# LayerNorm outputs transposed once in float32, and split after the transpose, from the fourth unit on

## The chip, the cores and the metric

The kernel runs on one core of a Trainium2 chip. The metric is the device time of one execution in microseconds. The kernel before the change takes 1624.39 us, the median of three runs (1623.93 to 1625.12).

The engines are named as the profile names them: PE (TensorE, with PEld for its weight loads), DVE (VectorE), ACT (ScalarE), POOL (GpSimd), SP (SyncE, which issues the transfers).

## The reference

Input `x` is 8 batches of 1024 tokens with 256 features in float32. With `LN` a LayerNorm without scale or shift:

```
x = x + LN(attention(LN(x), Wq, Wk, Wv, Wo))
x = x + LN(ffn(LN(x), weight, alpha, bias))

attention: q = x @ Wq (16 heads of 16), k = x @ Wk and v = x @ Wv (4 heads of 16, each used by 4 heads of q),
           rotary embedding of q and k, softmax(q k^T / sqrt(256)) v, then @ Wo
ffn:       x @ (ternary(weight) * alpha)^T + bias, where ternary gives 1, 0 or -1
           by a threshold of 0.7 * mean(|weight|)
```

## The kernel before

**Units.** The 8192 tokens are 16 units of 512 tokens (`UT` = 4 tiles of 128), two to a batch. A unit has three kinds of work: a projection (`Project`: LayerNorm of `x`, transposes, products for q, k and v, rotary embedding), the scores (32 steps of 4 score tiles, `SPU` = 32), and a tail (`Tail`: normalizing, the product with `Wo`, two LayerNorms, the ffn, the output). While the scores of unit u run, the tail of unit u-1 and the projection of unit u+3 are put between them.

**Scores.** For each of 128 score tiles of a unit TensorE makes `se` (L673, keys by queries), from which ScalarE takes the exponential `e` (L694), and `sm` (L600, queries by keys), of which VectorE takes the maxima `mx` (L625) for a later part of the scores. The products `av` (L714) add up `e` times v. `se` has three PSUM banks (`ps_e`), `sm` two double banks (`ps_mx`), `av` one.

**Windows.** `window` (L1164) takes two or three score tiles, with as many `sm` matmuls between, then stage parts that are due, then the `av` matmuls of a window two back. A part that needs a bank (`banked`, L1093) takes it from the three of `se`. So the size is 2 when such a part is ready and 3 otherwise (`window_size`, L1105), and a window of two does one such part. The order on PE, DVE and ACT is the order in which the program writes it (`manual_schedule`, L1253); POOL's is chosen by the scheduler. Each engine takes its queue in order. The steps at which parts come due stand in the lists `P_PARTS` (projection) and `T_PARTS`, `W_PARTS` (tail) from L969 on; `W_PARTS` is used for the tails 12 to 14, which run beside the scores of units 13 to 15.

**Two parts of float32.** Products are made in float32r, with each operand given as a rounded high part and the rest as a low part; a product adds high times high, high times low and low times high (`product`, L297; the ffn's weights are exact and need two terms). `split_hi` (L155) rounds, `split_lo` (L161) subtracts.

**The LayerNorm outputs** have to be transposed for the products. There are two ways in the kernel before:

- `transposed` (L262): GpSimd makes high and low part (L157, L162) of the normalized tile `xn`; then each part is transposed by four float32r matmuls (L267) into a bank, and ScalarE copies the bank to `xt0`, `xt1` or `ot0`, `ot1` (L271). Part `x` of `Project` and of `Tail` does this; there are four such parts for a projection (two halves, two parts each) and four for a tail.
- `transposed_split` (L274): `xn` is transposed once in float32 by four matmuls (L279), ScalarE copies the bank whole (L284), and GpSimd makes high and low part of the copy. Part `xw` of `Tail`, in `W_PARTS` alone.

In a projection the parts come from `begin` (L359: statistics, `norm`, `hi`, `lo`), and the transposed tiles are read by the products `pkv` and `pq`. The buffer `hl` (tag in `qkp`, one buffer) holds first the two parts `xs` of the projection's LayerNorm, then `hlq`, the two parts of the rotated q, which are sent to DRAM as `dq`. In a tail `scale` (L787, L788) and `heads` prepare the product `pa` with `Wo`; `stats_x` (L833) normalizes and splits; the product of the ffn is `pf`.

Other helpers that the prediction names: `kt` rotates k on GpSimd once `k_rot` has come back from DRAM; `rotate` (L312 to L317) and the splits of q run there too; `pm` (L648) transposes the maxima, and `ml` (L657) takes their low part from that bank.

Of the kernel before, what the change touches and what calls it, by code (L numbers as in the profile page):

```python
# [8 lines left out]
F32 = mybir.dt.float32  # L9
F32R = mybir.dt.float32r  # L10
# [6 lines left out]
P = 128  # L17
# [11 lines left out]
def kernel(  # L29
# [29 lines left out]
    nc = tc.nc  # L59
# [4 lines left out]
    ND = D // P  # L64
    NK = S // P
    UPB = S // UQ
    NU = B * UPB
# [8 lines left out]
    work = ctx.enter_context(tc.tile_pool(name="work", bufs=2))  # L76
# [78 lines left out]
    def split_hi(eng, hi, src):  # L155
        if eng is nc.gpsimd:
            eng.tensor_scalar(hi, src, 1.0, 0.0, ALU.mult, ALU.add)  # L157
        else:
            nc.scalar.copy(hi, src)

    def split_lo(eng, lo, src, hi):  # L161
        eng.tensor_tensor(lo, src, hi.bitcast(F32), ALU.subtract)  # L162

    def split(eng, hi, lo, src, hi_eng=None):

        split_hi(hi_eng or eng, hi, src)
        split_lo(eng, lo, src, hi)
# [15 lines left out]
    def psum(shape, name, dtype=F32):  # L183
        if spare[0]:
            spare[0] += 1
            if spare[0] % 5 < 2:
                return ps_mx.tile(shape, dtype, tag="sm", name=name)
        return ps_e.tile(shape, dtype, tag="se", name=name)
# [4 lines left out]
    ffn = {}  # L193
# [37 lines left out]
    def ln_stats(src):  # L231

        n = src.shape[1]
        mv = small.tile([P, 2, 2], F32, tag="mv", name="mv")[:, :n]
        st = small.tile([P, 2, 6], F32, tag="bnst", name="bnst")
        for t in range(n):
            nc.vector.bn_stats(st[:, t, :], src[:, t, :])  # L237
        for t in range(n):
            nc.vector.bn_aggr(mv[:, t, :], st[:, t, :])  # L239
        sc = small.tile([P, 2, 2], F32, tag="lnsc", name="lnsc")[:, :, :n]  # L240
        nc.gpsimd.tensor_scalar(sc[:, 1, :], mv[:, :, 1], EPS, 1.0, ALU.add, ALU.mult)  # L241
        nc.gpsimd.tensor_tensor(sc[:, 1, :], sc[:, 1, :], mhalf[:, :n], ALU.pow)  # L242
        nc.gpsimd.tensor_scalar(sc[:, 0, :], mv[:, :, 0], -1.0, 0.0, ALU.mult, ALU.add)
        return mv, sc
# [17 lines left out]
    def transposed(src, tag, name, copy=nc.scalar.copy):  # L262

        pt = psum([P, ND, 2 * P], f"pt_{name}", F32R)
        for t in range(2):
            for c in range(ND):
                nc.tensor.transpose(  # L267
                    pt[:, c, t * P : (t + 1) * P], src[:, t, c * P : (c + 1) * P], ident_r
                )
        dst = work.tile([P, ND, 2 * P], F32R, tag=tag, name=name, bufs=2 if tag[0] == "x" else 1)  # L270
        copy(dst, pt.bitcast(F32))  # L271
        return dst

    def transposed_split(src, tag, name):  # L274

        pt = psum([P, ND, 2 * P], f"pt_{name}")
        for t in range(2):
            for c in range(ND):
                nc.tensor.transpose(  # L279
                    pt[:, c, t * P : (t + 1) * P], src[:, t, c * P : (c + 1) * P], ident  # L280
                )

        whole = work.tile([P, ND, 2 * P], F32R, tag="xt0", name=name).bitcast(F32)
        nc.scalar.copy(whole, pt)  # L284
        parts = [
            work.tile([P, ND, 2 * P], F32R, tag=f"{tag}{l}", name=f"{name}_{l}", bufs=1)
            for l in range(2)
        ]
        split(nc.gpsimd, *parts, whole)
        return parts  # L290

    TERMS = ((0, 0), (0, 1), (1, 0))
# [19 lines left out]
    def rotate(eng, x, cos, sin, t2):  # L312

        for dst, table in ((t2, sin), (x, cos)):
            eng.tensor_tensor(dst, x, table.unsqueeze(1).to_broadcast(list(x.shape)), ALU.mult)  # L315
        eng.tensor_tensor(x[:, 0], x[:, 0], t2[:, 1], ALU.subtract)
        eng.tensor_tensor(x[:, 1], x[:, 1], t2[:, 0], ALU.add)  # L317
# [5 lines left out]
    class Project:  # L323
# [3 lines left out]
        def __init__(self, u, eng):  # L327
            self.u, self.eng = u, eng
            self.b, self.half = divmod(u, UPB)
            self.xt, self.sc, self.hl = {}, {}, {}  # L330
            self.q_rot = None
            if u not in (1, 2):
                xn = qkp.tile([P, UT, D], F32, tag="xn", name=f"xn_{u}", bufs=2)
                xs = qkp.tile([P, 2, UT, D], F32R, tag="hl", name=f"xs_{u}")
                self.xn = [xn[:, 2 * p : 2 * p + 2, :] for p in range(2)]
                self.xs = [[xs[:, l, 2 * p : 2 * p + 2, :] for l in range(2)] for p in range(2)]
            else:
                self.xn = [
                    tailp.tile([P, 2, D], F32, tag=f"xn{p}", name=f"xn_{u}_{p}") for p in range(2)
                ]  # L340
                self.xs = [
                    [ep.tile([P, 2, D], F32R, tag="e", name=f"xs_{u}_{p}_{l}") for l in range(2)]
                    for p in range(2)
                ]
# [14 lines left out]
        def begin(self, p):  # L359
            self.stats(p)  # L360
            self.norm(p)
            self.hi(p)
            self.lo(p)

        def x(self, p, l):
            self.xt[p, l] = transposed(self.xs[p][l], f"xt{l}", f"xt{l}_{self.u}_{p}")

        def kv(self, p):

            if p == 0:  # L370
                self.pkv = psum([P, UQ], f"pkv_{self.u}")
            xt = [self.xt[p, l] for l in range(2)]
            product(self.pkv[:, self.tokens(p)], columns(wqkv_s, D, 2 * DK), xt)
            if p == 1:
                self.kv_t = qkp.tile([P, UQ], F32, tag="kv_t", name=f"kv_t_{self.u}")
                nc.scalar.copy(self.kv_t, self.pkv)
# [361 lines left out]
    class Tail:  # L738
# [16 lines left out]
        def copy(self, p):  # L755
            return nc.scalar.copy
# [47 lines left out]
                self.copy(p)(hl[:, 0], self.on[p])  # L804
            split_lo(self.eng(p), hl[:, 1], self.on[p], hl[:, 0])

        def x(self, p, l):
            self.xt[p, l] = transposed(self.hl[p][:, l], f"ot{l}", f"ot{l}_{self.u}_{p}")

        def xw(self, p):  # L810
            self.xt[p, 0], self.xt[p, 1] = transposed_split(self.on[p], "ot", f"ot_{self.u}_{p}")

# [20 lines left out]
        def stats_x(self, p):  # L833
            self.sc[p] = ln_stats(self.x1[p])
            self.norm(p)
            if not NU - 4 <= self.u < NU - 1:
                self.split(p)

        def stats_f(self, p):
# [25 lines left out]
    class LastTail(Tail):  # L865
# [55 lines left out]
        x = o  # L921
# [17 lines left out]
    def at(step, f, *args):  # L939
        assert step >= -START  # L940
        todo.setdefault(step, []).append((f, args))
# [22 lines left out]
    def load(u):  # L964
# [2 lines left out]


    P_PARTS = (  # L969
        (26, "begin", 0), (33, "x", 0, 0), (34, "x", 0, 1), (37, "begin", 1), (43, "x", 1, 0),  # L970
        (45, "x", 1, 1), (49, "kv_and_dram"), (51, "q", 0), (54, "kt"), (53, "v"), (55, "q", 1),
        (62, "q_to_dram"),
    )
    L_PARTS = (
# [5 lines left out]
    T_PARTS = (  # L980
        (1, "fetch"), (7, "invert"), (8, "scale", 0), (9, "scale", 1), (12, "attn", 0),
        (15, "attn", 1), (15, "stats_a", 0), (17, "stats_a", 1), (19, "stats_x", 0),
        (23, "stats_x", 1), (24, "x", 0, 0), (25, "x", 0, 1), (26, "ffn", 0), (27, "x", 1, 0),
        (29, "x", 1, 1), (31, "ffn", 1), (31, "stats_f", 0), (33, "stats_f", 1),
    )


    P_SECOND = (26, 33, 34, 37, 43, 45, 49, 51, 52, 53, 55, 57)
    T_FIRST = (6, 8, 11, 12, 14, 16, 16, 17, 20, 23, 24, 25, 26, 27, 29, 31, 31, 33)
    P_FIRST = (47, 51, 52, 54, 57, 58, 59, 60, 62, 61, 63, 64)  # L990

    W_PARTS = (
        (1, "fetch"), (7, "invert"), (8, "scale", 0), (9, "scale", 1), (12, "attn", 0),
        (15, "attn", 1), (15, "stats_a", 0), (17, "stats_a", 1), (19, "stats_x", 0),
        (22, "xw", 0), (23, "stats_x", 1), (26, "ffn", 0), (27, "xw", 1), (31, "ffn", 1),
        (31, "stats_f", 0), (33, "stats_f", 1),
    )
    T_LAST = (1, 3, 4, 5, 9, 10, 11, 14, 17, 19, 20, 22, 25, 27, 24, 28)

    warm = []  # L1000
# [60 lines left out]
    for u in range(3, NU):  # L1061
        start = SPU * (u - 4)
        steps = P_FIRST if u == 3 else P_SECOND if u == 4 else [k for k, *_ in P_PARTS]
        at(start + steps[0] - 6, load, u)
# [12 lines left out]
    for u in range(NU - 1):  # L1077
        start = SPU * (u + 1)
        at(start + 1, begin_tail, u)
        parts = T_PARTS if u < NU - 4 else W_PARTS  # L1080
        steps = {0: T_FIRST, NU - 2: T_LAST}.get(u, [k for k, *_ in parts])
        for k, (_, *p) in zip(steps, parts):
            behind = [behind_latest] if u == 0 and p[0] == "fetch" else []
            at(start + k, *behind, part, tails, u, *p)
# [244 lines left out]
```

## Time and profile before

| what | value |
| --- | --- |
| median of three runs | 1624.39 us |
| the profiled execution: its time and its span | 1625.2 us |
| mean granted TensorE clock | 0.997 |
| steady unit (scores of unit 10, from 1039.19) | 96.30 us |
| unit 13 (no projection beside it, float32 transposes in its tail) | 90.57 us |
| `mx<-sm` reductions: 128x1024 | 715 of 1217 ns |
| `mx<-sm` reductions: 128x512 | 586 of 680 ns |
| `e<-se` exponentials | 1996 of 603 ns |
| ACT copies of a transposed bank: L271 to `xt`, to `ot`; L284 | 592, 599, 600 ns |
| POOL high part (L157) and low part (L162) of 128x512 | 621 and 1285 ns |

The profile is one execution, taken instruction by instruction. Busy time counts instructions in flight, waits between them not. Matmuls overlap: those of `se` and `sm` use different halves of the array's rows and run side by side, so TensorE's busy share says little about how close it is to its limit. A timeline row gives the start in us from the start of the span, the duration, the engine, the line, the operation, output<-inputs, the shape and the number of instructions merged into it; a bracket gives the idle time before it and what ended that.

### The profile page before, as it was taken

How to read it: one execution, taken by the hardware profiler on the slowest of the kernel's cores; microseconds unless marked ns; L12 is line 12 of the kernel's file. 1: busy time of each engine (PE TensorE's matmuls, PEld its weight loads, DVE VectorE, ACT ScalarE, POOL GpSimd, SP SyncE). 2: the span in 40 equal slices, each digit the busy share in tenths (PEclk: the TensorE clock that was granted, in tenths of full speed). 3: DMA queues.
4: the chain of work that ended last, by engine and by line, in shares of the span. 5: the costliest groups of instructions: out<-in, count | busy, mean ns of one | idle time of the engine just before them, and what ended most of it. 6: DMA issues, size and time to landing. Idle time of an engine off the chain costs nothing.

```text
span 1625.2 us, 37184 instructions
## 1 busy us (share of the span) xinstructions
PE 1576.5 (97%) x14702; PEld 813.9 (50%) x14702; DVE 1397.1 (86%) x2046; ACT 1270.1 (78%) x2473; POOL 833.8 (51%) x1239
## 2 busy tenths in 40 slices
PE   8999999999999999999999999999999999999997
PEld 6544454454545545454554545455454554444444
DVE  7878888889898888989889898988989888999964
ACT  4667878778787887878788787887878787787774
POOL 5542365364744637455364845546474552333354
PEclk9999999999999999999999999999999999999999
DMA  4151525124151422514133151513314141131100
GB/s 140 53 88 46 113 70 96 57 77 99 57 109 47 102 63 59 120 57 97 59 83 77 57 128 39 105 54 83 79 57 97 46 107 45 42 75 34 43 15 27
DMA packets 86078, 117.98 MB, mean 73 GB/s; under 512 B 12088, under 2 KB 50808, under 8 KB 85752
## 3 DMA queue, kind: packets, MB, share of 16 engines
q1 hardware_dynamic: 85904, 115.60, 29.7%
q8 instruction: 116, 1.90, 0.5%
q14 instruction: 58, 0.48, 0.1%
HBM read 68.65 MB, written 45.88 MB: 70 GB/s over the span
## 4 chain that ended last, share of the span: by engine, by line
PE 81%; DVE 10%; POOL 3%; ACT 2%; issue 2%; DMA 1%; SPq 0%; POOLq 0%; ACTq 0%; DVEq 0%
PE av L714 29%; PE se L673 28%; PE sm L600 9%; DVE mx L625 8%; PE pa L301 3%; PE pq L301 3%; PE pf L301 2%; ACT e L694 2%; PE pt_xt L267 2%; PE pt_ot L267 1%; PE pkv L301 1%; PE pm L648 1%; DVE bnst L237 1%; POOL lnsc L242 0%; DMA x<-in_L_attn_x 0%
## 5 line engine op out<-in xcount | busy, mean ns | idle before, releaser
L625 DVE TENSOR_REDUCE mx<-sm 128x2 f32<-128x1024 f32 (+1 forms) x1301 | 1204.8, 975 | 183.6 <-PE sm L600 164.0
L694 ACT ACTIVATE e<-se 128x512 f32<-128x512 f32 x1996 | 1057.0, 603 | 220.9 <-PE sm L600 163.7
L600 PE MATMUL sm<-k_st,q_st 64*128 64x512 f32 x2048 | 746.5, 448 | 7.2 <-DVE mx L625 4.1
L673 PE MATMUL se<-q_st,k_st 64*128 64x512 f32 x2048 | 705.6, 441 | 18.4 <-ACT e L694 14.6
L714 PE MATMUL av<-e,v_aug 128*32 128x256 f32 (+3 forms) x8584 | 606.0, 378 | 0.0
L673 PEld LDWEIGHTS se<-q_st,k_st 64*128 64x128 f32 x2048 | 324.5, 184 | 396.6 <-ACT e L694 305.4
L600 PEld LDWEIGHTS sm<-k_st,q_st 64*128 64x128 f32 x2048 | 325.2, 184 | 66.4 <-DVE mx L625 44.9
L714 PEld LDWEIGHTS av<-e,v_aug 128*32 128x32 f32 x8584 | 193.5, 108 | 212.5 <-issue 148.9
L241 POOL TENSOR_SCALAR lnsc<-mv 128x2 f32<-128x2 f32 (+1 forms) x134 | 26.1, 195 | 333.1 <-DVE mv L239 326.6
L788 POOL TENSOR_TENSOR xn<-xn,a 128x512 f32<-128x512 f32 x30 | 38.4, 1282 | 135.3 <-DMA a<-d_rec 130.0
L242 POOL TENSOR_TENSOR lnsc<-lnsc,mhalf 128x2 f32<-128x2 f32 (+1 forms) x134 | 92.5, 690 | 0.9
L157 POOL TENSOR_SCALAR xs<-xn 128x512 fp32r<-128x512 f32 x27 | 16.8, 621 | 130.8 <-DMA dq<-hlq 129.5
L162 POOL TENSOR_TENSOR hl<-xn,hl 128x512 fp32r<-128x512 f32 x54 | 68.7, 1285 | 0.1
L253 POOL TENSOR_SCALAR xn<-x,lnsc 128x256 f32<-128x256 f32 x116 | 64.3, 562 | 2.3
L853 POOL TENSOR_TENSOR a<-a,bias_bc 128x512 f32<-128x512 f32 x30 | 38.4, 1279 | 51.9 <-ACT a L852 51.9
L301 PE MATMUL pa<-woh,hl 128*128 128x256 f32 x240 | 46.2, 294 | 1.1 <-ACT e L694 1.1
L237 DVE BATCH_NORM_STATS2 bnst<-x 128x6 f32<-128x256 f32 x124 | 46.0, 413 | 1.3 <-DMA x<-in_L_attn_x 1.3
L315 POOL TENSOR_TENSOR t<-q_rot,sin_q_sb 128x512 f32<-128x512 f32 x31 | 39.7, 1282 | 12.2 <-ACT q_rot L457 12.1
L237 DVE BATCH_NORM_STATS2 bnst<-a 128x6 f32<-128x256 f32 x120 | 44.5, 413 | 0.0
L301 PE MATMUL pq<-xt,wqkvh 128*128 128x256 f32 x256 | 44.1, 294 | 0.5 <-ACT e L694 0.5
L457 ACT COPY q_rot<-pq 128x512 f32<-128x512 f32 x32 | 18.7, 586 | 28.3 <-PE pq L301 28.3
L301 PEld LDWEIGHTS pa<-woh,hl 128*128 128x128 f32 x240 | 34.6, 189 | 12.1 <-issue 6.3
(164 smaller groups left out, 1333.0 us busy)
## 6 DMA issues: line engine op xcount, KB each, us to landing
q_st<-dq SPq DMA_DIRECT2D x90, 256.0 KB
dq<-hlq SPq DMA_DIRECT2D x60, 256.0 KB
d_av<-avsb SPq DMA_DIRECT2D x60, 256.0 KB
x<-in_L_attn_x SPq DMA_DIRECT2D x15, 512.0 KB
xn<-d_av SPq DMA_DIRECT2D x30, 256.0 KB
a<-d_rec SPq DMA_DIRECT2D x30, 256.0 KB
xr<-in_L_attn_x SPq DMA_DIRECT2D x15, 512.0 KB
out_x<-a SPq DMA_DIRECT2D x30, 256.0 KB
```

Of the source, the lines that this page charges most:

```text
L162: eng.tensor_tensor(lo, src, hi.bitcast(F32), ALU.subtract)
L237: nc.vector.bn_stats(st[:, t, :], src[:, t, :])
L242: nc.gpsimd.tensor_tensor(sc[:, 1, :], sc[:, 1, :], mhalf[:, :n], ALU.pow)
L253: eng.tensor_scalar(dst[:, t, :], src[:, t, :], sc[:, 0, t : t + 1] if eng is nc.gpsimd else mv[:, t, 0:1], sc[:, 1, t : t + 1], ALU.add i ...
L267: nc.tensor.transpose(pt[:, c, t * P : (t + 1) * P], src[:, t, c * P : (c + 1) * P], ident_r)
L301: nc.tensor.matmul(out, chunk(left[i], c), chunk(right[j], c), start=(k == 0), stop=(k == len(steps) - 1),)
L315: eng.tensor_tensor(dst, x, table.unsqueeze(1).to_broadcast(list(x.shape)), ALU.mult)
L600: scores = nc.tensor.matmul(sm[0][:, part, :], queries[rows], k_st[(u // UPB) % 3][rows, r2, ch * 512 : (ch + 1) * 512], start=True, stop= ...
L625: early[0] = nc.vector.tensor_reduce(mx[i][:, a, head_and_tile(i, r2, t), lo:n], sm[0][:, lo:n, :], AX.X, ALU.max).ins
L673: nc.tensor.matmul(sc if len(queries.shape) == 2 else sc.rearrange("p (j t) -> p j t", j=G), k_st[(i // G // UPB) % 3][rows, r2, kt * P : ...
L694: nc.scalar.activation(e, sc, AF.Exp, scale=1.0 / D**0.5)
L714: nc.tensor.matmul(av_ps[0][32 * r : 32 * r + 32, lo:hi], va[:, kt, r, :], es[i * NK + kt, r // 2, r % 2][:, lo:hi], start=(kt == 0 and lo ...
```

## The change

From projection 3 on, and in all tails but the last, the normalized tile is transposed once in float32 (`transposed_split`, part `xw`). ScalarE now copies the bank twice: rounded into the high part, and whole. The whole copy goes back into the memory of the tile that was transposed, viewed by its new axes, and not into a buffer of tag `xt0`. GpSimd then only subtracts. `begin` no longer splits; projections from the fourth on have no `xs`, so `hl` holds `hlq` alone there. `W_PARTS` becomes the list of all tails, and the projection's list has two `xw` parts in place of four `x` parts. In a tail the first transposes come due at step 22, where `x` had steps 24 and 25; the second at 27, where `x` had 27 and 29.

```diff
@@ transposed_split
-        whole = work.tile([P, ND, 2 * P], F32R, tag="xt0", name=name).bitcast(F32)
-        nc.scalar.copy(whole, pt)
         parts = [
-            work.tile([P, ND, 2 * P], F32R, tag=f"{tag}{l}", name=f"{name}_{l}", bufs=1)
+            work.tile(
+                [P, ND, 2 * P], F32R, tag=f"{tag}{l}", name=f"{name}_{l}",
+                bufs=2 if tag[0] == "x" else 1,
+            )
             for l in range(2)
         ]
-        split(nc.gpsimd, *parts, whole)
+        whole = src.rearrange("p (c t) d -> p c (t d)", c=ND)
+        nc.scalar.copy(parts[0], pt)
+        nc.scalar.copy(whole, pt)
+        split_lo(nc.gpsimd, parts[1], whole, parts[0])
         return parts
@@ Project.begin
             self.stats(p)
             self.norm(p)
-            self.hi(p)
-            self.lo(p)
...
+        def xw(self, p):
+            self.xt[p, 0], self.xt[p, 1] = transposed_split(self.xn[p], "xt", f"xt_{self.u}_{p}")
@@ Tail.stats_x
-            if not NU - 4 <= self.u < NU - 1:
+            if self.u == NU - 1:
                 self.split(p)
@@ P_PARTS
-        (26, "begin", 0), (33, "x", 0, 0), (34, "x", 0, 1), (37, "begin", 1), (43, "x", 1, 0),
-        (45, "x", 1, 1), (49, "kv_and_dram"), (51, "q", 0), (54, "kt"), (53, "v"), (55, "q", 1),
+        (26, "begin", 0), (33, "xw", 0), (37, "begin", 1), (43, "xw", 1),
+        (49, "kv_and_dram"), (51, "q", 0), (54, "kt"), (53, "v"), (55, "q", 1),
         (62, "q_to_dram"),
@@ T_PARTS
-        (23, "stats_x", 1), (24, "x", 0, 0), (25, "x", 0, 1), (26, "ffn", 0), (27, "x", 1, 0),
-        (29, "x", 1, 1), (31, "ffn", 1), (31, "stats_f", 0), (33, "stats_f", 1),
+        (22, "xw", 0), (23, "stats_x", 1), (26, "ffn", 0), (27, "xw", 1), (31, "ffn", 1),
+        (31, "stats_f", 0), (33, "stats_f", 1),
@@ first units
-    P_SECOND = (26, 33, 34, 37, 43, 45, 49, 51, 52, 53, 55, 57)
-    T_FIRST = (6, 8, 11, 12, 14, 16, 16, 17, 20, 23, 24, 25, 26, 27, 29, 31, 31, 33)
-    P_FIRST = (47, 51, 52, 54, 57, 58, 59, 60, 62, 61, 63, 64)
+    P_SECOND = (26, 33, 37, 43, 49, 51, 52, 53, 55, 57)
+    T_FIRST = (6, 8, 11, 12, 14, 16, 16, 17, 20, 22, 23, 26, 27, 31, 31, 33)
+    P_FIRST = (47, 51, 54, 57, 59, 60, 62, 61, 63, 64)
@@ main loop
-        parts = T_PARTS if u < NU - 4 else W_PARTS
+        parts = T_PARTS
```

More of the change, by code (lines that the diff above doesn't have):

```diff
@@ L333, in __init__ @@
                 xn = qkp.tile([P, UT, D], F32, tag="xn", name=f"xn_{u}", bufs=2)
+                self.xn = [xn[:, 2 * p : 2 * p + 2, :] for p in range(2)]
+            if u == 0:
                 xs = qkp.tile([P, 2, UT, D], F32R, tag="hl", name=f"xs_{u}")
-                self.xn = [xn[:, 2 * p : 2 * p + 2, :] for p in range(2)]
                 self.xs = [[xs[:, l, 2 * p : 2 * p + 2, :] for l in range(2)] for p in range(2)]
-            else:
+            elif u < 3:
                 self.xn = [
@@ L805, in split @@
             split_lo(self.eng(p), hl[:, 1], self.on[p], hl[:, 0])
-        def x(self, p, l):
-            self.xt[p, l] = transposed(self.hl[p][:, l], f"ot{l}", f"ot{l}_{self.u}_{p}")
         def xw(self, p):
@@ L982 @@
         (15, "attn", 1), (15, "stats_a", 0), (17, "stats_a", 1), (19, "stats_x", 0),
-        (23, "stats_x", 1), (24, "x", 0, 0), (25, "x", 0, 1), (26, "ffn", 0), (27, "x", 1, 0),
-        (29, "x", 1, 1), (31, "ffn", 1), (31, "stats_f", 0), (33, "stats_f", 1),
-    )
-    P_SECOND = (26, 33, 34, 37, 43, 45, 49, 51, 52, 53, 55, 57)
-    T_FIRST = (6, 8, 11, 12, 14, 16, 16, 17, 20, 23, 24, 25, 26, 27, 29, 31, 31, 33)
-    P_FIRST = (47, 51, 52, 54, 57, 58, 59, 60, 62, 61, 63, 64)
-    W_PARTS = (
-        (1, "fetch"), (7, "invert"), (8, "scale", 0), (9, "scale", 1), (12, "attn", 0),
-        (15, "attn", 1), (15, "stats_a", 0), (17, "stats_a", 1), (19, "stats_x", 0),
         (22, "xw", 0), (23, "stats_x", 1), (26, "ffn", 0), (27, "xw", 1), (31, "ffn", 1),
```

## The prediction

> **What bounds the kernel now.** First the page's shares, to see which engines are near full.
>
> ```profile
> span 1625.2 us, 37184 instructions
> PE 1576.5 (97%) x14702; PEld 813.9 (50%) x14702; DVE 1397.1 (86%) x2046; ACT 1270.1 (78%) x2473; POOL 833.8 (51%) x1239
> PE 81%; DVE 10%; POOL 3%; ACT 2%; issue 2%; DMA 1%; SPq 0%; POOLq 0%; ACTq 0%; DVEq 0%
> ```
>
> The third line is the chain of waits: TensorE carries 81% of it and VectorE 10%. But matmuls overlap, so 97% busy does not say that TensorE never waits. The stretches show what is behind it. The first two below are whole units of 32 steps in the steady part (the score units 10 and 13; unit 13 has no projection left to do).
>
> ```profile
> 1039.19:1135.49 96.30, 94.83 (x920) 48.73 (x916) 85.13 (x124) 78.21 (x153) 53.25 (x78) 1.00 0.32 78
> 1328.09:1418.66 90.57, 88.10 (x849) 42.50 (x846) 82.30 (x119) 72.44 (x142) 30.56 (x46) 1.00 0.25 56
> ```
>
> The columns are span, then busy time of PE, PEld, DVE, ACT, POOL. Unit 13 has far less matmul work, and still takes 90.57 us with VectorE busy for 82.30. So TensorE and VectorE bound the kernel by turns: VectorE while nothing but scores runs, TensorE where a stage's matmuls come between. Units 2 to 12 take 96.30 to 96.45 us each.
>
> By turns, because the work goes in windows: two or three `se` matmuls paired with as many `sm` matmuls, at most one stage part (if two), then the `av` group. I read a window in TensorE's timeline from its first `se` row to the next window's. Windows of three without a wait last 1.46 us (`av` of one 256-wide piece) or 1.68 (one of 384, or two pieces); over units 3 to 14 their mean is 0.20 longer, up to 2.40. There VectorE reduces without a break and TensorE waits for a bank. Where small windows with parts follow one another, VectorE starves:
>
> ```profile
> 1074.23 1.22 DVE L625 TENSOR_REDUCE mx<-sm 128x2 f32<-128x1024 f32 x1 [0.20 <-PE sm L600]
> 1076.22 1.23 DVE L625 TENSOR_REDUCE mx<-sm 128x2 f32<-128x1024 f32 x1 [0.76 <-PE sm L600]
> 1079.07 1.23 DVE L625 TENSOR_REDUCE mx<-sm 128x2 f32<-128x1024 f32 x1 [1.62 <-PE sm L600]
> 1080.77 4.68 DVE L625 TENSOR_REDUCE mx<-sm 128x2 f32<-128x1024 f32 x5 [0.47 <-PE sm L600]
> ```
>
> The windows of 1073.43 to 1079.96 hold a transpose, a product `pa` and another transpose; the brackets add up to 3.05 us of idle VectorE. The change takes out windows like these.
>
> **The change part by part, for a unit like 10** (tail 9 and projection 13 run in it).
>
> *Transposes.* Eight groups of four in float32r become four groups in float32. Groups of both kinds stand in TensorE's timeline, each followed by its `av` row:
>
> ```profile
> 1114.92 0.54 PE L267 MATMUL pt_ot<-ident_r,hl 128*128 128x128 f32 x4
> 1115.39 0.85 PE L714 MATMUL av<-e,v_aug 128*32 128x384 f32 x8
> ...
> 1396.16 0.66 PE L279 MATMUL pt_ot<-ident,xn 128*128 128x128 f32 x4
> 1396.75 0.86 PE L714 MATMUL av<-e,v_aug 128*32 128x256 f32 x16
> ```
>
> Start to start, 0.47 us (0.45 to 0.47 in others; I take 0.46) against 0.59. So 8 x 0.46 - 4 x 0.59 = **-1.32 us**. The weight loads of the two kinds take the same, 140 ns each by their groups (L267 and L279 for `pt_ot`).
>
> The Trainium skill (TensorE: Matmul & The Clock Gate, Weight-path perf modes) speaks against the float32 form: the fast weight load, about 2x as measured there, is used only for 128 weights of a type that is not FP32. If float32r counted as such a type, a load of float32 would take twice 140 ns; 16 loads would add 16 x 0.14 = 2.2 us to a unit, an estimate by that page, and the change would lose. The two equal rows decide against it here.
>
> *Windows.* In the instruction order of the changed kernel units 1 to 12 have 49 windows (30 of three, 19 of two) where the trace has 50 (28 and 22). A group of `av` takes 0.57 us with one 256-wide piece and 0.78 otherwise: 22 x 0.57 + 28 x 0.78 = 34.4 before, 19 x 0.57 + 30 x 0.78 = 34.2 after. Each window also pays at its start and its end about 0.1 us more between score pairs than inside (0.34 and 0.33 against 0.23). Together **-0.35 us**, -0.15 to -0.5.
>
> *What VectorE takes back.* Two windows more are of three, and those run at VectorE's pace: 2 x 0.20 = **+0.4 us**, from 0 (if each lands where VectorE is starved) to +1.0. Over the whole kernel the order has 7 more reductions, each a split of one into two: 7 x (2 x 0.680 - 1.217) = 1.0 us, inside these bounds.
>
> *The bank.* The transposes' bank, one of three for `se`, is now held for two ScalarE copies (0.59 and 0.60 us) instead of one, before the third `se` of the next window can have it. ScalarE's copies number the same: 8 per unit. In the two `pt_xt` windows at 1044.80 and 1048.40 the copy ends at 1046.89 and 1050.55; one copy more makes 1047.48 and 1051.14, against a third `se` at 1047.30 and 1050.67, which the longer transposes push 0.13 later: 0.05 and 0.34 us late. Queued behind these copies are the window's next exponentials. Four times 0.1 gives **+0.4**, 0 to 4 x 0.34 = +1.4.
>
> *GpSimd.* Four high-part copies (0.62) go per unit: 2.5 us. Subtractions (1.28) stay four, now behind the transposes. The wait `xs` <- DMA of `hlq` (12.3 us in this unit) goes with the shared buffer; GpSimd sits off TensorE's path there, so I count it at nothing, and next in line after it is `a` L853, ready early. But in the second half of the unit GpSimd is packed, and the tail's first transposes come earlier on TensorE (step 22 instead of 24, ahead of the second `pq`):
>
> ```profile
> 1099.14 0.73 POOL L315 TENSOR_TENSOR t2k<-k_rot,sin_kt_sb 128x256 f32<-128x256 f32 x1 [2.65 <-DMA k_rot<-d_k]
> ...
> 1108.01 1.11 POOL L253 TENSOR_SCALAR xn<-x,lnsc 128x256 f32<-128x256 f32 x2
> ```
>
> From the DMA's landing GpSimd works in one run until `xn` is there, at 1109.12, 19.5 us after the window with `pkv` began (1089.65). Summing the windows of the new order up to the transposes by the rows of before (3.23, 1.68, 1.63, 3.29, 1.68, 1.61, 2.0, 1.5, 1.75, and 0.67 inside the last) TensorE is there after 19.0. It would wait 0.5 us, and all behind it on its queue too, the second `pq` first. Part of that falls where VectorE sets the pace: **+0.2**, 0 to +0.8. The subtraction behind it is due for `pf`, nine to ten us later, and is hidden: the copies and the subtraction take 0.6 + 0.6 + 1.3. The projection's subtractions have three or more windows before `pkv` needs them. If that cover went, `pf` or `pkv` would wait on GpSimd.
>
> *SyncE* issues the same 737 transfers; only `hlq` of unit 3 goes out earlier. Nothing is late by it.
>
> Sum per unit: -1.32 - 0.35 + 0.4 + 0.4 + 0.2 = -0.67. The other ledger is VectorE's idle time, 11.2 us in the unit. Without the second transposes the cluster quoted above should keep 0.20 + 0.76 + 0.8 = 1.8 of 3.05; the pair of `pt_ot` windows (0.54 + 0.68 idle) becomes one beside `pq`: together with `ptv` and that `pq` 2.9 becomes 1.9; the first `pt_xt` pair gives 0.3. That is -2.5, and the same givebacks plus 4 x 0.13 for longer transposes make +1.1: -1.4. The ledgers bracket it; I take **-1.0 us per unit**. Units 1 to 12 have it: -12. Unit 0 has the projection of unit 3 alone: 4 x 0.46 - 2 x 0.59 = -0.7. Units 13 to 15 already transpose in float32, keep their 46, 47 and 42 windows, and trade a GpSimd copy for one on ScalarE: 0. Span 1625.2 - 12.7 = 1612.5. The span is 0.8 us above the median of 1624.39, so I forecast **1612 us**.
>
> **The rivals.**
> *A, the whole of it.* VectorE refills fully and no giveback comes: 2.2 us per unit, 26.4 + 0.7: 1597. For it: the idle ledger. Against it: the bank and `xn`.
> *B, swallowed.* Windows of three are already paced by VectorE, so TensorE's saving becomes waiting: for it unit 13: by the windows' shortest forms it has 78.6 us of TensorE against 89.5 in unit 10, and these 10.9 us less gave 5.7 us of time, in part because VectorE's busy time fell by 2.8. Against it: 11.2 us of idle VectorE, at windows that go. Then 1623.
> *C, slower.* GpSimd's run gets `xn` to the tail's first transposes late, and TensorE, in order, waits in each of 12 units. At the 0.2 us I take nothing turns; it decides from 1.2 us per unit on. At 2.2 us (the `k_rot` wait was up to 3.6 long against 2.65 here, one us more; one more if `pkv` is reached later by the chain than I sum) the unit grows by 1.0: 1624.4 + 12 - 0.7 = 1636. For it: the packed rows from 1099.14 on. Against it: the hand sum gives only 0.5.
> That the change does not do what it says is excluded by the instruction order: 16 float32 transposes stand per unit where 32 float32r stood.
>
> **How the numbers follow.** Forecast (1604 to 1619) 0.45, A 0.27, B 0.13, C 0.15. About 0.2%, 3.2 us, is what a measurement of this kernel can tell from no change: faster is 0.45 + 0.27 = 0.72, same 0.13, slower 0.15. The range goes from A to just beyond B, 1597 to 1625.
>
> **What would show it.** Per steady unit: span about 95.3; VectorE busy near 85 still, its idle near 10; four groups of L279-like transposes 0.59 from start to `av`; no wait of `xs` for `hlq`. Wrong, if `pt_ot` or `pf` waits for GpSimd by more than 1 us per unit (C), if the third `se` after transposes waits near 0.6 us for the second copy, or if the unit falls below 94.5 (A).

## The result and the profile after

The changed kernel takes **1633.3 us** (median of four, 1630.5 to 1634.1) against 1624.6 for the kernel before in the same session: ratio 1.0049, 95% interval 1.0035 to 1.0063. It is slower by 0.5%, more than the measurement's own uncertainty. The forecast was 1612.

First the same three lines of the page, after (its execution took 1630.5 us):

```profile
span 1628.6 us, 36757 instructions
PE 1573.8 (97%) x14470; PEld 797.0 (49%) x14470; DVE 1396.1 (86%) x2053; ACT 1272.5 (78%) x2479; POOL 805.0 (49%) x1183
PE 71%; DVE 20%; POOL 3%; issue 2%; DMA 2%; ACT 2%; SPq 0%; POOLq 0%; DVEq 0%; ACTq 0%
```

TensorE has 232 matmul records fewer and GpSimd 56 instructions fewer, as meant. But in the chain of waits VectorE's share went from 10% to 20%, and TensorE's from 81% to 71%: the chain now passes through VectorE more often. What that is worth in time the chain does not say; the units do. The two stretches of one unit each, after (score units 10 and 13):

```profile
1042.34:1138.76 96.42, 94.70 (x904) 47.48 (x901) 85.14 (x125) 78.17 (x153) 51.20 (x74) 1.00 0.32 78
1331.72:1422.29 90.57, 88.02 (x840) 42.24 (x836) 82.08 (x119) 73.10 (x144) 29.39 (x44) 1.00 0.26 57
```

Unit 10 was 96.30 and is 96.42. VectorE's idle time there was 96.30 - 85.13 = 11.17 and is 96.42 - 85.14 = 11.28: the forecast wanted 1.4 less. Unit 13 stayed, as forecast. The cluster that the prediction quoted, in VectorE's timeline after:

```profile
1077.57 1.23 DVE L631 TENSOR_REDUCE mx<-sm 128x2 f32<-128x1024 f32 x1 [0.20 <-PE sm L606]
1079.67 1.22 DVE L631 TENSOR_REDUCE mx<-sm 128x2 f32<-128x1024 f32 x1 [0.87 <-PE sm L606]
1082.53 4.68 DVE L631 TENSOR_REDUCE mx<-sm 128x2 f32<-128x1024 f32 x5 [1.64 <-PE se L679]
```

The brackets add up to 2.71 us (3.05 before; 1.8 forecast). The window with the second transposes is gone, but the 1.6 us of idle time after the product `pa` was never that window's: it stays and stands before the next window of three.

**By units.** I read each unit's length as the time from its first `se` to the next unit's (unit 0 from TensorE's first matmul, at 3.92 us in both):

| score unit | before | after | difference |
|---|---|---|---|
| 0 | 166.51 | 163.28 | -3.23 |
| 1 | 98.16 | 103.23 | +5.07 |
| 2 | 96.32 | 96.40 | +0.08 |
| 3 to 12 together | 963.18 | 964.88 | +1.70 |
| 13 and later | 297.1 | 296.9 | -0.2 |

So there are two questions: what costs 5 us in unit 1, and why the other eleven of the twelve units that should have gained 1 us each gained nothing. (Unit 0 turns out to be the clock's, see below; without its 3.2 us the spans would differ by 6.6 us, and the medians differ by 8.7; the two us between are within what executions of either kernel differ by.)

**Unit 1.** TensorE's timeline after has two long waits there, which the kernel before doesn't have:

```profile
192.68 0.47 PE L679 MATMUL se<-q_st,k_st 64*128 64x512 f32 x1 [3.67 <-DMA q_st<-ml]
...
242.50 0.98 PE L279 MATMUL pt_ot<-ident,xn 128*128 128x128 f32 x4 [2.56 <-POOL xn L253]
```

The first waits for the shift rows of job 5 (the maxima for one part of the scores, put beside the queries), which a DMA brings from `ml` into `q_st`. The timeline of SyncE's queue, after and then before, says what went out ahead of them:

```profile
177.23 6.62 SPq L496 DMA_DIRECT2D dq<-hlq  x4
185.12 1.48 SPq L670 DMA_DIRECT2D q_st<-ml  x2
```

```profile
188.05 1.39 SPq L664 DMA_DIRECT2D q_st<-ml  x2
...
211.45 4.55 SPq L490 DMA_DIRECT2D dq<-hlq  x4
```

The queries of unit 3 (four transfers of 256 KB) moved from behind the shift rows to just ahead of them. In the stretches 170 to 180 and 180 to 190 us the DMA engines are busy to 0.98 and 0.77 (before: 0.75 and 0.93). Why they moved stands in GpSimd's timeline of the kernel before:

```profile
210.22 1.20 POOL L157 TENSOR_SCALAR hlq<-q_rot 128x512 fp32r<-128x512 f32 x2 [1.33 <-PE pt_xt L267]
```

`hlq` of unit 3 could not be written before the transposes had read `xs` of projection 4, for both live in the one buffer `hl`. The change frees that buffer, GpSimd writes `hlq` at 169.2 to 177.4, and its transfers go out into engines that are full.

### The profile page after: what moved, and what is told of

Same layout as the page of the kernel before. It is cut to its first block, busy times and chain, and to the rows that moved or that the text cites. A ratio compares the mean times of both kernels' runs of the same rounds, so it can differ in the third digit from the quotient of the medians.

```text
span 1628.6 us, 36757 instructions
## 1 busy us (share of the span) xinstructions
PE 1573.8 (97%) x14470; PEld 797.0 (49%) x14470; DVE 1396.1 (86%) x2053; ACT 1272.5 (78%) x2479; POOL 805.0 (49%) x1183
## 4 chain that ended last, share of the span: by engine, by line
PE 71%; DVE 20%; POOL 3%; issue 2%; DMA 2%; ACT 2%; SPq 0%; POOLq 0%; DVEq 0%; ACTq 0%
PE av L720 25%; PE se L679 23%; DVE mx L631 17%; PE sm L606 9%; PE pa L305 3%; PE pq L305 3%; PE pf L305 2%; PE pkv L305 1%; ACT e L700 1%; DVE bnst L237 1%; PE pt_ot L279 1%; PE pt_xt L279 1%; PE pm L654 1%; DMA q_st<-ml 0%; DMA k_rot<-d_k 0%
## 5 line engine op out<-in xcount | busy, mean ns | idle before, releaser
L679 PE MATMUL se<-q_st,k_st 64*128 64x512 f32 x2048 | 712.9, 443 | 10.2 <-ACT e L700 4.2
L720 PE MATMUL av<-e,v_aug 128*32 128x256 f32 (+2 forms) x8552 | 603.6, 379 | 0.0
L162 POOL TENSOR_TENSOR xt<-xn,xt 128x512 fp32r<-128x512 f32 x26 | 33.5, 1290 | 69.2 <-ACT xn L292 69.2
L162 POOL TENSOR_TENSOR ot<-xn,ot 128x512 fp32r<-128x512 f32 x30 | 38.5, 1285 | 58.9 <-ACT xn L292 58.7
L733 ACT COPY avsb<-av 128x512 f32<-128x512 f32 x63 | 37.9, 601 | 5.4 <-PE av L720 5.4
L162 POOL TENSOR_TENSOR hlq<-q_rot,hlq 128x512 fp32r<-128x512 f32 x31 | 39.8, 1283 | 3.1 <-ACT hlq L159 0.7
```

The lines of the kernel that those rows point to most:

```text
L679: nc.tensor.matmul(sc if len(queries.shape) == 2 else sc.rearrange("p (j t) -> p j t", j=G), k_st[(i // G // UPB) % 3][rows, r2, kt * P : ...
L720: nc.tensor.matmul(av_ps[0][32 * r : 32 * r + 32, lo:hi], va[:, kt, r, :], es[i * NK + kt, r // 2, r % 2][:, lo:hi], start=(kt == 0 and lo ...
```

## The experiments

Runs that stand without an interval (e3, e4, e8 to e14, e17, e18) were measured once, and every unit length is read from one profile of its run.

Theory at the start: unit 1 loses by these two waits; the steady units gain nothing because VectorE's pace swallows TensorE's saving (the forecast's rival B). Rivals: ScalarE's second copy takes the saving; `xn` from GpSimd is late in every unit (rival C).

**Unit 1, one wait at a time.**

```diff
# e1
-    P_FIRST = (47, 51, 54, 57, 59, 60, 62, 61, 63, 64)
+    P_FIRST = (47, 51, 54, 57, 59, 60, 62, 61, 63, 76)
...
+            late = ("kt", "q_to_dram") if u > 4 else ("q_to_dram",) if u == 3 else ()
+            behind = [behind_latest] if p[0] in late else []
# e2
-    T_FIRST = (6, 8, 11, 12, 14, 16, 16, 17, 20, 22, 23, 26, 27, 31, 31, 33)
+    T_FIRST = (6, 8, 11, 12, 14, 16, 16, 17, 20, 24, 24, 26, 27, 31, 31, 33)
```

> The changed kernel with one thing moved: the four transfers of `dq` of unit 3 (out of `hlq`) go out behind the shift rows `q_st` of job 5 on SyncE's queue, as before the change. Theory (unit 1 pays 3.7 us because these transfers stand ahead of `q_st` in DMA engines that are 77 to 98% busy): window `se_4_7_0_1` loses its wait of 3.67 us for the transfer of `q_st`, unit 1 falls from 103.2 to about 99.5 us and the time from 1633 to about 1629.5; a wait of about 1.3 us for the next `q_st`, as in the kernel before, may come back, which leaves 1631. Rival (the four transfers only happen to be near, and the rows are late because unit 0 is 3.2 us shorter): the wait stays at 3 us or more and the time within 1 us of 1633. The steady units stay at 96.4 by both.

> The changed kernel with the first transposes of tail 0 at step 24 instead of 22, behind the second `pq` of projection 4. Theory (GpSimd has `xn` of tail 0 ready 2.56 us after TensorE asks for it, since two `hlq` instructions and `pow` stand between): the wait goes below 0.5 us, unit 1 falls from 103.2 to 100.5 to 101.5 and the time by 1.7 to 2.6, to about 1631. Rival (TensorE's lateness there is covered by VectorE, which sets the pace behind it): the wait goes, the time stays within 0.7 us of 1633. The 3.67 us for `q_st` stay.

e1: 1631.0, ratio to before 1.0041 (1.0024 to 1.0058); unit 1 101.64. The wait of 3.67 us went, as expected, but the unit fell by 1.6 us only: the wait for `xn` grew to 2.90, and in it and behind it the clock was at half. Stretches of 1 us of e1; the first number after the engines' busy times is the granted clock:

```profile
238.00:239.00 1.00, 0.54 (x3) 0.29 (x3) 0.00 (x0) 0.00 (x0) 0.94 (x2) 0.50 0.49 133
...
242.00:243.00 1.00, 1.00 (x5) 0.80 (x4) 0.65 (x1) 0.97 (x2) 0.16 (x1) 0.50 0.00 0
243.00:244.00 1.00, 1.00 (x6) 1.00 (x6) 1.00 (x3) 0.00 (x0) 0.00 (x0) 0.50 0.43 33
```

The window with the second `pq`, behind the wait, took 4.32 us where it took 2.85 in the changed kernel. e2: 1631.2, ratio 1.0042 (1.0026 to 1.0057); unit 1 101.99. The `xn` wait went, the waits for shift rows stayed (5.0 us in two). Each move alone gives little, since the other wait remains and grows. Together:

> The changed kernel with both moves: the four `dq` transfers of unit 3 behind the shift rows of job 5, and the first transposes of tail 0 at step 24, behind the second `pq` of projection 4. Each alone left the other's wait in unit 1, and a long wait of TensorE was followed by some 4 to 6 us at half the granted clock. Theory (the loss of the change lies in unit 1 alone, the steady units are worth nothing): no wait over 2 us and no half clock in unit 1, unit 1 near 98.2 us as before the change, unit 0 at 163.2, units 2 to 12 at 96.4; the time is that of the kernel before less 3.2 in unit 0 and plus 12 x 0.12, 1623 against 1625, ratio 0.998 to 1.000. Rival (lateness of unit 1 has further causes): unit 1 stays above 100 and the ratio above 1.001.

e5: 1627.4, ratio 1.0011 (1.0001 to 1.0022). Unit 1 is 96.14, 7.1 us shorter than in the changed kernel; unit 2 is 97.48, 1.1 longer, as one `pf` of tail 0 now falls into it. Of TensorE's waits for others in units 1 and 2 the longest left is 1.3 us, and the granted clock is 1.00 from 24 to 1540 us:

```profile
PE se L679 <- ACT e L700: 1.4, 3, 0.5
PE se L679 <- DMA q_st<-ml: 1.3, 1, 1.3
```

So the loss in unit 1 is these two waits and the clock behind the first. Steady units stay at 96.4, as expected. The ratio was expected at 0.998 to 1.000 and missed that narrowly. Undone, the loss leaves a kernel that is about level with the one before, not a faster one.

**Unit 0.**

> The kernel before, unchanged, for a second profile. In the first one the granted clock fell to half twice in unit 0 (near 28 and near 105 us), and in the profile of the kernel before with its parts spread, whose unit 0 has the same instructions, it did not, and unit 0 took 162.65 us instead of 166.51. Theory (the 3.2 us that unit 0 gained in the changed kernel's profile are the clock's, not the change's): a profile without such a drop shows unit 0 at 162.5 to 163.5 and a span near 1621.5. Rival (the change shortens unit 0): unit 0 stays at 166 or more though the clock is full.

Unit 0 took 165.0 in this profile, with one of the two drops of the clock (half from 23.8 to 30.7 us) and full clock at 100 to 108; with no drop it had taken 162.65 (e7 below, same unit 0), with both 166.51. The expectation's case without any drop didn't come up here, but the three profiles of the same instructions follow the clock. Without a drop, unit 0 took 162.65 to 163.11 with the old instructions (e7, e12, e14) and 162.88 to 163.28 with the new (the changed kernel, e1, e2, e5). The 3.2 us are not the change's.

**What swallows the saving.** The maxima are reduced over part of the columns, so VectorE's reductions get shorter and nothing else:

```diff
# e3 on the kernel before, e4 on the changed one (256 of 512)
-                mx[i][:, ::-1, head_and_tile(i, r2, t), ch], sm[0], AX.X, ALU.max
+                mx[i][:, ::-1, head_and_tile(i, r2, t), ch], sm[0][:, :, :256], AX.X, ALU.max
...
-            mx[i][:, a, head_and_tile(i, r2, t), lo:n], sm[0][:, lo:n, :], AX.X, ALU.max
+            mx[i][:, a, head_and_tile(i, r2, t), lo:n], sm[0][:, lo:n, :256], AX.X, ALU.max
```

> The kernel before, with VectorE's maxima reduced over the first 256 of each 512 scores only (the other half of the scores is left out of the shift). With VectorE's reductions cut to near half, it no longer paces windows, so this shows the time that TensorE and the other waits alone need. Both theories: below 1624, between 1540 and 1600.

> The changed kernel with the same shortened maxima (the other half of the scores is left out of the shift). Theory (TensorE's 1.3 to 1.7 us per unit are saved, but VectorE's pace and the bank of the transposed maxima swallow them): steady units are 1.2 to 1.8 us shorter than with the kernel before so shortened. Rival 1 (ScalarE's second copy out of the bank takes the saving): the steady units are within 0.5 us of that, or longer. Rival 2 (`xn` late from GpSimd in every unit): `pt_ot` waits for `xn` by more than 1 us in each unit here, and the units are longer.

One steady unit of each, e3 and then e4, in the columns of above:

```profile
905.24:998.19 92.95, 91.83 (x921) 46.91 (x918) 54.83 (x124) 77.62 (x153) 53.33 (x78) 1.00 0.33 82
```

```profile
810.96:902.04 91.08, 90.85 (x905) 45.50 (x901) 54.66 (x124) 77.30 (x153) 51.23 (x74) 1.00 0.35 84
```

With VectorE at 55 us instead of 85 the change is worth 1.9 us in this pair of units. On the mean of units 3 to 12 it is worth 1.6 (93.14 and 91.55), as some units of e4 wait for shift rows. Forecast were 1.67 for transposes and windows, before what is taken back. The saving is real; unit 1 was 104.9 in e4 and ate half of it (1556.5 against 1566.5).

**Does spreading the parts help?** I took VectorE's idle time for a matter of parts that stand side by side:

```diff
# e6 (on e5)
-        (26, "begin", 0), (33, "xw", 0), (37, "begin", 1), (43, "xw", 1),
-        (49, "kv_and_dram"), (51, "q", 0), (54, "kt"), (53, "v"), (55, "q", 1),
+        (26, "begin", 0), (33, "xw", 0), (37, "begin", 1), (41, "xw", 1),
+        (49, "kv_and_dram"), (51, "q", 0), (54, "kt"), (54, "v"), (57, "q", 1),
...
-        (22, "xw", 0), (23, "stats_x", 1), (26, "ffn", 0), (27, "xw", 1), (31, "ffn", 1),
+        (23, "xw", 0), (23, "stats_x", 1), (27, "ffn", 0), (29, "xw", 1), (31, "ffn", 1),
```

e7 moves the parts of the kernel before likewise: the second tile pair's `x` to 41 and 42, `v` to 54, the second `q` to 57, and in tails `x` to 24, 26, 28 and 29 and the first `ffn` to 27.

> As the run with both moves, and in all units from 5 on the second `pt_xt` two steps earlier, away from `pm` and `pa`; `ptv` one step later, away from `pm`; `pt_ot` one and two steps later, the second `pq` two steps later, away from `pt_ot`, the first `pf` one step later. The number of windows is unchanged (49, 30 of three). Theory (VectorE's idle time comes in clusters where parts stand in adjacent windows, and TensorE's saving is swallowed by VectorE in the runs of three between them): spread, VectorE's idle time falls from 11.2 to about 9.5 per unit and steady units from 96.4 to 94.5 to 95.5, time 1604 to 1616. Rival (the pace is set by VectorE's busy time and its fixed hand-overs, not by where the parts stand): units within 0.4 of 96.4, time within 5 us of the run with both moves.

> The kernel before (eight float32r transposes groups per unit) with its parts spread by the same steps. Theory (TensorE's saving of 1.3 to 1.9 us per unit counts once the parts no longer starve VectorE in clusters): spreading alone gives less than spreading with the change: steady units 0.5 to 1.5 longer than with the change spread. Rival (the transposes are worth nothing whatever the places): within 0.3 of it.

Theory and rival missed in both: e6 took 1651.0, ratio 1.0168 (1.0145 to 1.0192), and e7 1644.3, ratio 1.0108 (1.0090 to 1.0126). Steady units took 97.1 to 99.6 and 97.4 to 97.7. In e6 VectorE's long idle times just moved with the parts (1.91 and 1.86 us behind `pa` and `pq` in unit 10), and the wait for shift rows came into nearly every unit. Two rows of its waits, with total, times and longest:

```profile
PE sm L606 <- DVE mx L631: 15.0, 37, 1.4
PE se L679 <- DMA q_st<-ml: 13.5, 12, 1.9
```

**More TensorE, less VectorE, less ScalarE**, each on e5:

```diff
# e9
-        for t in range(2):
+        for t in range(4):
+            t = t % 2
# e10
-        for t in range(n):
-            nc.vector.bn_stats(st[:, t, :], src[:, t, :])
+        nc.vector.bn_stats(st[:, 0, :], src[:, 0, :])
         for t in range(n):
-            nc.vector.bn_aggr(mv[:, t, :], st[:, t, :])
+            nc.vector.bn_aggr(mv[:, t, :], st[:, 0, :])
# e11
-        nc.scalar.copy(whole, pt)
```

> The run with both moves, with each of the four float32 transpose groups of a unit written twice into its bank: TensorE has 16 transposes more per unit, some 4 x 0.55 = 2.2 us. Theory (VectorE sets the pace where the transposes stand, so TensorE's time there counts for little in either direction): steady units 96.4 to 97.3. Rival (each us of TensorE counts, and the saving was lost by other costs of the change, such as ScalarE's second copy): 98.3 to 98.8.

> The run with both moves, with the first-pass statistics of the LayerNorms taken of one of each two tiles only (the other tile gets the same mean and variance): VectorE loses 8 of 17 `bnst` instructions per unit, 8 x 0.41 = 3.3 us, and TensorE's work stays. Theory (VectorE's pace): steady units 93.4 to 95.2, 1 to 3 us shorter. Rival (VectorE's idle time just grows): 96.0 or more.

> The run with both moves, without ScalarE's second copy of the bank (`whole` then keeps the untransposed values, so that the low parts are left out in effect): 4 copies of 0.61 us less per unit on ScalarE, and the bank free 0.6 us earlier. Theory A (ScalarE's second copy, by its time or by holding the bank, takes TensorE's saving): steady units 95.0 to 95.9 instead of 96.4. Theory B (the saving is lost since the groups that went away stood in windows that VectorE's backlog covered, and the longer float32 groups are paid in full): 96.1 to 96.4.

One steady unit of e9, of e10 and of e11:

```profile
1052.74:1150.88 98.14, 96.40 (x920) 49.24 (x916) 85.14 (x125) 78.50 (x153) 51.16 (x74) 1.00 0.32 77
```

```profile
1036.98:1133.12 96.14, 94.69 (x904) 47.51 (x901) 82.87 (x117) 78.09 (x153) 51.20 (x74) 1.00 0.34 78
```

```profile
1040.64:1137.09 96.45, 94.67 (x905) 47.50 (x901) 85.07 (x125) 76.22 (x149) 51.05 (x74) 1.00 0.34 79
```

e9 speaks against the theory: 1.74 us more in this unit (2.0 on the mean of units 3 to 12), in full, for each of the four transpose windows grew by 0.43 to 0.45 (2.04 to 2.48 the first). e10 too: VectorE has 2.2 us less to do and the unit is 0.25 shorter; on the mean of units 3 to 12 VectorE's idle time grows from 11.4 to 13.3 us. So "VectorE's pace", as a rule for all of its work and in both directions, is wrong. e11 decides against ScalarE's second copy: without it ScalarE has 1.9 us less to do and the bank is free 0.6 us earlier, and the unit is as long as before (96.45).

**One part alone.** The new transposes in one part of the kernel before only: in projections from unit 5 on (e12), in tails 1 to 11 (e13), or for the second pair of tiles of a projection (e14, the last two lines of e12's diff alone).

```diff
# e12
-        (33, "x", 0, 0), (34, "x", 0, 1),
+        (33, "xw", 0),
...
-        (43, "x", 1, 0), (45, "x", 1, 1),
+        (43, "xw", 1),
# e13
-        (24, "x", 0, 0), (25, "x", 0, 1),
+        (22, "xw", 0),
...
-        (27, "x", 1, 0), (29, "x", 1, 1),
+        (27, "xw", 1),
```

> The kernel before, with the new transposes in the projections alone, from unit 5 on (their steps as in the changed kernel); tails as before. Of the changed kernel's stretches, the one with the first `pt_xt` got 0.5 us longer, the one with `pt_xt` beside `pa` 0.5 shorter. Theory B: steady units 96.0 to 96.5. If each us of TensorE counted everywhere: 95.6.

> The kernel before, with the new transposes in the tails alone, of units 1 to 11; projections as before. Theory B: steady units 96.0 to 96.5 by the sums over the changed kernel's windows; if each us of TensorE counted everywhere: 95.6.

> The kernel before, with the new transposes for the second pair of tiles of a projection alone, from unit 5 on: the one place where the changed kernel's windows gained, since VectorE is starved there (`pa` stands beside it). Theory B: the best of these runs, steady units 95.6 to 96.0. Rival (the place does not matter, a saving is always swallowed): 96.3 or more.

All three missed every expectation: 1669.5, 1670.0 and 1665.8, steady units 98.7 to 103.4. They are inconclusive for the question, for they brought waits that neither kernel has. In e12:

```profile
PE se L681 <- DMA q_st<-ml: 38.0, 12, 4.5
```

In e13 that wait is 21.5 us and `pt_ot` waits 12.4 for `xn`; in e14 `pt_xt` waits 13.4 for `xs`, and `sm` 15.4 for VectorE. Half of this change is far worse than all of it, and these rows point to what comes late from SyncE's and GpSimd's queues. Which of the moved instructions does it I did not settle.

**How far is the kernel from the point where the saving counts?** The last four: 256 columns on e5 and on the kernel before, and 448 of 512 columns on both (the diff as for e3 with 448).

> The run with both moves of unit 1, with the maxima reduced over 256 of each 512 scores (the other half is left out of the shift). It shows the change without its loss in unit 1 and without VectorE's pace. Theory (TensorE's saving is real and counts once VectorE's reductions are short): steady units near 91.0, unit 1 at 96 or less, time 1544 to 1552. Rival (the shorter units of the earlier run came from that run's own luck): 1556 or more.

> The kernel before with the same shortened maxima, as the partner of that run on the same chip. Theory: steady units 92.9 to 93.0, time 1566, 15 to 22 above the partner. Rival: less than 8 above it.

> The kernel before with the maxima reduced over 448 of each 512 scores (an eighth is left out of the shift): VectorE loses some 9 of 76 us of reductions per unit. Theory (VectorE paces the runs of windows of three): steady units 94 to 96.

> The run with both moves and maxima over 448 of each 512 scores (an eighth is left out of the shift). Theory (kernel before and after stand at a point where VectorE's reductions are just the slower ones, so a small relief already lets the saving through): steady units 0.8 to 1.9 shorter than with the kernel before so relieved. Rival (the reductions have to shrink by much more): less than 0.4 shorter.

e15: 1549.7, ratio to before 0.9509 (0.9462 to 0.9556); e16: 1563.1, 0.9608 (0.9573 to 0.9643). The intervals lie apart: with short reductions the change, with both moves, gains 13.4 us, 0.9%. That is a little under the theory's 15 to 22 and well over the rival's 8. Undisturbed steady units: 92.93 in e16, 91.2 in e15 (some of its units have up to 0.8 more; waits for shift rows come to 11.2 us over the run). With 448 columns, e17 (shorter than the 94 to 96 expected) and e18 (0.8 shorter than e17, at the lower end of what the theory expected):

```profile
1009.30:1102.80 93.50, 92.50 (x920) 49.00 (x917) 77.77 (x124) 77.81 (x153) 53.29 (x78) 1.00 0.34 80
```

```profile
906.62:999.30 92.68, 92.41 (x904) 47.98 (x900) 77.72 (x125) 77.93 (x153) 51.15 (x74) 1.00 0.32 81
```

| columns reduced | undisturbed steady unit, old transposes | new | difference | difference of the means of units 3 to 12 |
|---|---|---|---|---|
| 512 | 96.30 | 96.39 to 96.42 | +0.1 | +0.1 to +0.2 |
| 448 | 93.47 | 92.68 | -0.8 | -0.85 |
| 256 | 92.94 | 91.1 to 91.2 | -1.7 to -1.9 | -1.4 to -1.6 |

An eighth off VectorE's reductions lets half of the saving through, half off lets nearly all of it through. In the chain of waits VectorE's share falls with it, from 10% and 20% (before, after) to 3% and 5% in e17 and e18. This shows that the reductions hold the steady units: they stand on the path, since a bank for `sm` comes free only through them.

TensorE's timeline shows where the reductions hold it. Cut into windows as in the prediction, on the mean of units 3 to 12, the 30 windows of three of the kernel with both moves take 53.61 us with all columns and 50.87 with 448; the 28 of the kernel before take 49.47 and 47.50. The window with `ptv` (the transposes of v) falls from 2.36 to 1.96 with the new transposes and stays at 1.46 to 1.47 with the old. So in these windows the relief gives the new kernel 1.2 us more than the old one, and on the whole unit 0.9 more.

The statistics don't hold the units; most of what e10 left out became idle time of VectorE, so it was not on the path. e9 fits too, if both engines are near their limits: what is added in a transpose window (2.04 us for two scores) comes on top, and what is taken away is met by the reductions. That last step is argued from e9 and the table together and not shown by itself.

The kernels with shortened maxima are faster than both, e15 by 4.9%. They shift by a maximum over part of the scores. The shift cancels in the quotient, but a score left out may exceed it, so the exponent isn't bounded for every input as it is with the full maximum. With the full maximum, and nothing else left out, no version here beat the kernel before.

## Why the prediction was wrong

- *Transposes -1.32, windows -0.35.* Right as TensorE's time. The groups take 0.59 from start to `av` in float32 too (fence below), there are 49 windows, and with half the columns reduced the unit is 1.4 to 1.6 shorter on the mean, 1.7 to 1.9 where it is undisturbed.

```profile
1113.05 0.66 PE L279 MATMUL pt_ot<-ident,xn 128*128 128x128 f32 x4
1113.64 0.86 PE L720 MATMUL av<-e,v_aug 128*32 128x256 f32 x16
```

- *What VectorE takes back, +0.4.* **This term failed in the steady units.** It priced only the two more windows of three, 0.20 each. Measured: about 1.8, the 1.67 that transposes and windows save and the 0.1 by which the unit grew; as far as the relieved runs show, it lies in the windows of three and in the one with `ptv`. The second ledger, 2.5 us of idle VectorE gone, was the same mistake: it took each idle time for the work of the window in front of it, and 11.17 became 11.28. The row that spoke for it was in the prediction: unit 13 has 10.9 us less TensorE and is only 5.7 us shorter, which was read for rival B and given 0.13.
- *The bank, +0.4.* Nothing: e11.
- *`xn` late, +0.2.* Nothing in the steady units, and the sums were good: `xn` done 19.5 us after the window with `pkv` began (19.5 forecast), TensorE there after 19.3 (19.0). In unit 1, which was not summed, 2.6 us. In GpSimd's timeline after, unit 10:

```profile
1103.21 0.73 POOL L319 TENSOR_TENSOR t2k<-k_rot,sin_kt_sb 128x256 f32<-128x256 f32 x1 [2.95 <-DMA k_rot<-d_k]
...
1112.12 1.10 POOL L253 TENSOR_SCALAR xn<-x,lnsc 128x256 f32<-128x256 f32 x2
```

- *SyncE: only `hlq` of unit 3 goes out earlier, "Nothing is late by it".* **This step failed in unit 1.** The forecast saw the move and did not look at what stands behind it on the queue: shift rows that TensorE needs 4 us after their issue, in a stretch with a DMA share of 0.75 to 0.93 in the trace of before. It cost 3.67 us and half clock after it.
- *GpSimd's wait for the buffer, counted at nothing.* Its time shows in no steady unit; its effect on the order does in unit 1. That wait held the four transfers back.
- *Unit 0, -0.7.* Not seen: between executions without a drop of the clock there, old and new lie within 0.6 us of each other. The clock's drops are worth up to 3.9 us.
- *Units 13 to 15, 0.* Right: 90.56 to 90.57 and 91.41 to 91.45 in the first two, -0.2 for all that is left from unit 13 on.
- *Rivals.* B has the steady units (it forecast 1623; e5, without the loss in unit 1, took 1627.4, and its profiled execution 1623.5). C's wait is real, once. No rival had a transfer that comes too early.

## What to carry to other kernels

When two engines share the pace, price a saving at the slower one's instructions on the path (here the reductions that free a bank), not at either engine's idle time; shortening that engine's work in a run for measurement shows whether there is anything to win. When a change frees a buffer, list the transfers that the buffer held back and look at what stands behind them on the queue and how full the DMA engines are then.

## What was not expected of the hardware

**The clock.** After the wait of 3.67 us in unit 1 the granted clock stayed full for one more us and then went to half for 3.4 us (stretches of the changed kernel):

```profile
192.00:193.00 1.00, 0.33 (x3) 0.34 (x5) 0.00 (x0) 0.00 (x0) 0.00 (x0) 1.00 1.07 347
193.00:194.00 1.00, 1.00 (x14) 0.38 (x10) 0.55 (x1) 0.82 (x2) 0.00 (x0) 0.82 0.64 174
194.00:195.00 1.00, 1.00 (x10) 0.44 (x4) 1.00 (x2) 0.75 (x2) 0.00 (x0) 0.50 0.24 83
...
197.00:198.00 1.00, 1.00 (x10) 0.56 (x6) 1.00 (x3) 0.72 (x2) 0.00 (x0) 0.97 0.00 0
```

In e1 the clock fell to half two us into the wait of 2.90 us and stayed there for 6.8 us. The wait of 2.56 us in the changed kernel had no drop. In the kernel before 3.4 us at half came right behind a wait of only 1.00 us at 102 us, while the same wait in the changed kernel, at 100 us, had none. In the clock records of all these traces every drop but the last one of a trace lasts 3.4 us or a multiple of it (6.8 us in e8, 10.2 in unit 1 of e4). The Trainium skill (TensorE: Matmul & The Clock Gate, Part 1: The HAM clock gate) says that the clock halves after an idle window of about 3.4 us and comes back after about as much busy time, and that the window runs freely, so the phase counts. The 3.67 us and the recovery agree; the drops at 2.90 and 1.00 us come sooner than it says. For a kernel like this it means that unit 0 alone moved by 3.9 us between executions of the same instructions, more than many changes are worth.
